# A recurrence beside attention on one core: the framework's scheduler, or the kernel's own list schedule

## The chip, the core and the metric

The kernel runs on one core of a Trainium2 chip. A core has five engines, each with its own queue of instructions that are started in the order of the queue: PE (TensorE, matmuls, with weight loads listed apart as PEld), DVE (VectorE), ACT (ScalarE), POOL (GpSimd) and SP (SyncE, which here only issues DMAs). They meet at semaphores. The metric is device time in microseconds of one execution; lower is better.

## The reference, cut to what matters

The input is eight images of 56 x 56 pixels with 256 channels, fp32. Layer 0 normalizes by groups and runs attention between regions of 8 x 8 pixels: each of an image's 49 regions picks 4 regions by the product of pooled queries and keys, keeps the best 32 of 256 scores for every pixel, takes a softmax over them, adds a depthwise convolution and projects. Layer 1 runs attention in a window of 7 tokens, and then a recurrence over the 3136 tokens of each image:

```python
def step(carry, xs):
    h, c = carry
    xi_t, xf_t, xg_t, xo_t = xs
    i_t = jax.nn.sigmoid(xi_t + h @ V_i)
    f_t = jax.nn.sigmoid(xf_t + h @ V_f)
    g_t = jnp.tanh(xg_t + h @ V_c)
    o_t = jax.nn.sigmoid(xo_t + h @ V_o)
    c_new = h * c + i_t * g_t
    h_new = o_t * jnp.tanh(c_new)
    return ((h_new, c_new), h_new)
```

The new cell state is `h * c + i_t * g_t`, so the gate f is never used: three gates (i, c, o) are computed. All 3136 steps depend on each other; the eight images form the batch of a step. Every residual is added.

## The kernel before, in words

**Order of the program.** An image is seven rows of seven regions; the kernel goes through `rows`, all eight images at row p before row p + 1. For the row at hand it emits seven `region`s, and between them the pieces of a list `todo`: the projection and window attention of the row before it (`project`, `window_attention`), the queries and convolution of the row after it (`queries_and_lepe`) and, while p is 0, the statistics, routing, keys and values of the next image (`norm_and_route`).

**Region (L367 to L448).** SP reads the four chosen places from a table in on-chip memory and issues eight gathers (kg, vg). PE computes scores (`sc`, L399). For each of four groups DVE takes four rounds of the eight largest (`max`, L411) and their removal (`match_replace`, L412), ACT exponentiates (L417), DVE masks and sums (L419), ACT divides (L424), PE transposes (L427), ACT copies (L430), and PE multiplies with the values (`av`, L435).

**Gate terms.** `gates(i)` of `window_attention` multiplies 112 normalized tokens of an image with the input weights (L605), adds the bias on POOL in one instruction of 768 columns (L610), and stores them in memory (`xg`).

**Recurrence (L682 on).** Blocks of 16 steps. The state h lies with channels on partitions, 2 x 8 columns. A step multiplies h, as the stationary operand, with V (L704): the output has the eight images on 8 rows of each of four groups of 32 partitions, so four groups of columns are in work at once. Gates i and c go to one PSUM bank (`r_pic`, 128 columns), gate o to another (`r_po`, 64 columns). ACT has copied the gate terms there beforehand (`place_terms`, L678, two steps at a time), and the matmuls add to them. Then come:

- `r_tic`: DVE transposes i and c (L710); `r_ig`: their tanh on ACT (L712). Sigmoids are made of tanh by halved weights.
- `r_to`, `r_og`: the same for gate o (L714, L716).
- `r_m` and `r_c`: two DVE operations for the new cell state (L719, L724); `r_tc`: its tanh (L726).
- `r_hs`: the new h on DVE (L729); `r_hc`: POOL's product of h and c for the next step (L732).

At the end of a block PE transposes the 16 states (L739), DVE adds the residual (L743), SP stores the result. Terms are loaded eight steps at a time into two buffers (`r_gin`).

**What sets the order.** The Tile framework records the program, and its scheduler reorders the instructions of each engine. The recurrence of a row of tokens can begin when all eight images have stored their gate terms, so its steps are queued when row p, image 1, is reached. `advance` then emits a fixed number of step pieces after each region, at a higher priority (offset 3000):

```python
            rate = -(-len(steps) // (NWIN * nb))
        for qi in range(NWIN):
            ...
            if steps:
                advance(rate)
```

The last 560 steps have no attention left beside them.

Of the kernel before, what the change touches and what calls it, by code (L numbers as in the profile page):

```python
# [8 lines left out]
F32 = mybir.dt.float32  # L9
# [30 lines left out]
SLOTS = 4  # L40
PRIORITY = 3000
# [7 lines left out]


# [5 lines left out]
def _halve(nc, t, views):  # L56


    for v in views:
        for g in (0, 2):  # L60
            w = v.rearrange("p (j g u) -> p j g u", g=GATES, u=UJ)[:, :, g, :]
            nc.vector.tensor_scalar(w, w, 0.5, None, ALU.mult)
# [3 lines left out]
def _layers(ctx: ExitStack, tc, a, out):  # L66
# [96 lines left out]

    def norm_and_route(b, im):
# [42 lines left out]
        def route():  # L209
# [29 lines left out]
            im["kd"] = dram.tile([NREG, P, 2 * S], F32, name=f"kd{b}")  # L239
            im["vd"] = dram.tile([N, C], F32, name=f"vd{b}")  # L240

        def keys_values(p):
# [31 lines left out]
        return (  # L274
            [lambda p=p: stats(p) for p in range(NWIN)]
            + [groups, route]
            + [lambda p=p: keys_values(p) for p in range(NWIN)]
# [9 lines left out]
    def queries_and_lepe(b, p, im, row):  # L287
# [63 lines left out]
        def convolve(m):  # L351
            pl = bank()
            for dx in range(3):
                for g in range(4):
                    nc.tensor.matmul(  # L355
                        pl[g * HD : (g + 1) * HD, :ROW], diag[:, m, dx, g, :],
                        row["vs"][:, m, g, :, dx : dx + W],
                        start=(dx == 0), stop=(dx == 2), skip_group_check=True,
                    )
# [5 lines left out]
        return [  # L365
            queries,
            lambda: (values(0), shift(0)),  # L367
            lambda: (values(1), shift(1)),
            lambda: convolve(0),
            lambda: convolve(1),  # L370
        ]

    def region(n, qi, im, row):


        _, regs = nc.values_load_multi_w_load_instructions(
            im["idx"][n : n + 1, 0:TOPK], engines=[SP], min_val=0, max_val=NREG - 1,
            skip_runtime_bounds_check_because="max_index returns places in 49 columns",
        )
        kg = work.tile([P, TOPK, 2, S], F32, name="kg")  # L380
        vg = work.tile([P, 2, C], F32, name="vg")
        for j, reg in enumerate(regs):
            nc.sync.dma_start(
                kg[:, j].rearrange("p k s -> p (k s)"),
                im["kd"][bass.ds(reg, 1)].rearrange("o p s -> p (o s)"),
            )
            nc.sync.dma_start(
                vg[(j % 2) * S : (j % 2 + 1) * S, j // 2, :], im["vd"][bass.ds(reg * S, S), :]
            )
# [4 lines left out]
        for pair in range(2):  # L394
            both = ps_sc.tile([P, 2, 512], F32, name="sc")
            for g2 in range(2):
                rows = slice((2 * pair + g2) * HD, (2 * pair + g2 + 1) * HD)
                for k in range(2):
                    nc.tensor.matmul(  # L399
                        both[k * S : (k + 1) * S, g2, :KEYS],  # L400
                        row["q"][rows, k, qi * S : (qi + 1) * S],
                        kg[rows, :, k, :], start=True, stop=True,
                    )
# [28 lines left out]
        for k in range(2):  # L432
            for jj in range(2):
                for g in range(4):
                    nc.tensor.matmul(  # L435
                        av[g * HD : (g + 1) * HD, k, :],
                        vg[:, jj, k * P + g * HD : k * P + (g + 1) * HD],
                        probs[g][:, jj, k * S : (k + 1) * S],
                        start=(jj == 0), stop=(jj == 1), skip_group_check=True,
                    )  # L440
# [23 lines left out]
    def project(b, p, im, row):  # L464
# [47 lines left out]
        return [begin] + [lambda i=i: block(i) for i in range(NQB)] + [end]  # L512

    def window_attention(b, p, im, row):
# [83 lines left out]
        def gates(i):  # L598
# [11 lines left out]
            nc.gpsimd.tensor_tensor(gs, gs, bu, ALU.add)  # L610
# [5 lines left out]
        return (  # L616
# [3 lines left out]
            + [lambda i=i: gates(i) for i in range(lo, hi)]  # L620
# [13 lines left out]
    t2 = [dram.tile([QB, nb, C], F32, name=f"t2d{n}") for n in range(NBLK)]  # L634
# [8 lines left out]
    for t in state.values():  # L643
        nc.vector.memset(t, 0.0)
# [235 lines left out]
```

## Time and profile before

| | |
|---|---|
| median of 3 runs | 12276.32 us (12260.72 to 12298.11) |
| profiled execution | 12274.44 us, its span 12272.7 us |
| mean granted PE clock | 0.764 of full |
| busy: PE, DVE, ACT, POOL | 77%, 75%, 44%, 18% |
| first r_hs, last r_hs | 1707.9 us, 12267.9 us |

Busy time is the union of an engine's instructions. Consecutive instructions on one engine overlap a little, and matmuls overlap much, so a mean duration times a count can exceed the busy time. Idle time of an engine counts only where it holds up the chain that ends last. A line of an instruction view gives start, duration, engine, line, operation, output<-inputs, shapes and, in brackets, the idle time before it and who ended it.

### The profile page before, as it was taken

The page shows a single profiled execution, that of the slowest core. Times are in us where ns is not written, and L with a number is a line of the kernel's source. Part 1 is how long each engine was busy: PE and PEld are TensorE (multiplying, and loading weights), DVE is VectorE, ACT ScalarE, POOL GpSimd, SP SyncE. Part 2 cuts the span into 40 slices and gives each one's busy share as a digit, 9 for nine tenths or more (in the row PEclk, how much of TensorE's full clock was granted, in tenths as well). Part 3 has the DMA queues.
Part 4 walks back from the last instruction along what each step waited for, and adds up shares of the span by engine and source line. Part 5 has one row for each costly group of instructions (what it writes and reads, how often), then busy time and mean ns, then how long its engine had stood idle before and what let it go on. Part 6 is the DMA issues. An engine that isn't in the chain of part 4 may idle for free.

```text
span 12272.7 us, 376190 instructions
## 1 busy us (share of the span) xinstructions
PE 9402.1 (77%) x135660; PEld 5455.3 (44%) x135660; DVE 9147.9 (75%) x43038; ACT 5428.8 (44%) x20193; POOL 2178.0 (18%) x6148
## 2 busy tenths in 40 slices
PE   6777778887888887888888887788888888655555
PEld 3344344444444444444444444444444444433333
DVE  5767688888888888888888888888888888533333
ACT  2333344444455444444544444444445444322222
POOL 2222112111122121121211211211112121100000
PEclk8787778777888788787888778887778888755555
DMA  4343322222222222222222222222222222100000
GB/s 135 93 116 99 98 57 61 57 58 58 60 62 57 55 58 55 58 56 54 57 56 59 55 53 59 56 56 57 55 58 56 56 58 53 31 16 17 17 16 15
DMA packets 785586, 705.72 MB, mean 58 GB/s; under 512 B 106403, under 2 KB 755705, under 8 KB 783721
## 3 DMA queue, kind: packets, MB, share of 16 engines
q1 hardware_dynamic: 783720, 681.66, 20.7%
q8 instruction: 1072, 17.56, 0.6%
q14 instruction: 794, 6.50, 0.2%
HBM read 421.58 MB, written 179.83 MB: 49 GB/s over the span
## 4 chain that ended last, share of the span: by engine, by line
PE 48%; DVE 33%; ACT 8%; issue 6%; DMA 2%; POOL 2%; SPq 1%; ACTq 0%; DVEq 0%; POOLq 0%
PE r_pic L704 16%; DVE left L412 9%; DVE top L411 7%; PE r_po L704 6%; PE mm L605 3%; PE pt L427 3%; PE sc L399 3%; DVE r_hs L729 3%; DVE pe L419 3%; DVE r_to L714 3%; PE mm L355 2%; PE av L435 2%; PE mm L532 2%; DVE r_tic L710 2%; DVE r_c L724 2%
## 5 line engine op out<-in xcount | busy, mean ns | idle before, releaser
L704 PE MATMUL r_pic<-r_v,r_hs 128*8 128x128 f32 x50160 | 2599.4, 336 | 1609.2 <-DVE r_hs L729 1593.3
L704 PEld LDWEIGHTS r_pic<-r_v,r_hs 128*8 128x8 f32 x50160 | 1229.0, 100 | 3038.0 <-DVE r_hs L729 2490.0
L710 DVE STREAM_TRANSPOSE r_tic<-r_pic 128x128 f32<-128x128 f32 x3136 | 977.7, 312 | 1439.2 <-PE r_pic L704 1410.2
L712 ACT ACTIVATE r_ig<-r_tic 128x32 f32<-128x32 f32 x3136 | 714.7, 228 | 2999.3 <-DVE r_tic L710 2904.6
L412 DVE MATCH_REPLACE8 left<-top,left 128x256 f32<-128x256 f32 x4704 | 1908.8, 407 | 0.4
L411 DVE MAX8 top<-left 128x8 f32<-128x256 f32 x4704 | 1895.5, 412 | 3.3 <-issue 0.2
L732 POOL TENSOR_TENSOR r_hc<-r_hs,r_c 128x16 f32<-128x16 f32 x3136 | 725.6, 231 | 6255.0 <-DVE r_hs L729 5870.9
L704 PE MATMUL r_po<-r_v,r_hs 128*8 128x64 f32 x50160 | 1655.7, 262 | 0.0
L704 PEld LDWEIGHTS r_po<-r_v,r_hs 128*8 128x8 f32 x50160 | 1334.4, 111 | 161.2 <-issue 0.2
L427 PE MATMUL pt<-ident,pe 128*128 128x128 f32 x3136 | 837.8, 354 | 441.2 <-ACT pe L424 421.5
L399 PE MATMUL sc<-kg,q 32*64 32x256 f32 x6272 | 969.5, 488 | 182.9 <-ACT pe L417 175.1
L417 ACT ACTIVATE pe<-sc,nmax 128x256 f32<-128x256 f32 x1568 | 742.7, 474 | 708.9 <-DVE left L412 473.0
L424 ACT ACTIVATE pe<-pe,inv 128x256 f32<-128x256 f32 x1568 | 787.0, 502 | 549.3 <-DVE inv L423 546.0
L726 ACT ACTIVATE r_tc<-r_c 128x16 f32<-128x16 f32 x3136 | 669.7, 214 | 701.4 <-DVE r_c L724 592.1
L729 DVE SCALAR_TENSOR_TENSOR r_hs<-r_og,r_tc 128x16 f32<-128x16 f32 x3136 | 605.6, 193 | 367.8 <-ACT r_tc L726 347.7
L435 PE MATMUL av<-pts,vg 128*32 128x64 f32 x12544 | 699.2, 264 | 206.8 <-ACT pts L430 167.6
L714 DVE STREAM_TRANSPOSE r_to<-r_po 128x64 f32<-128x64 f32 x3136 | 728.6, 232 | 134.7
L411 DVE MAX8 top<-sc 128x8 f32<-128x256 f32 x1568 | 660.9, 421 | 212.3 <-PE sc L399 172.0
L605 PE MATMUL mm<-wu,xlT 128*112 128x512 f32 (+1 forms) x1792 | 777.9, 557 | 19.5 <-ACT xlT L600 13.9
L430 ACT COPY pts<-pt 128x256 f32<-128x256 f32 x1568 | 579.0, 369 | 468.8 <-PE pt L427 454.9
L427 PEld LDWEIGHTS pt<-ident,pe 128*128 128x128 f32 x3136 | 409.0, 169 | 840.7 <-ACT pe L424 644.3
L415 POOL TENSOR_SCALAR nmax<-top 128x1 f32<-128x1 f32 x1568 | 341.5, 218 | 2299.2 <-DVE top L411 1120.1
(141 smaller groups left out, 14563.1 us busy)
## 6 DMA issues: line engine op xcount, KB each, us to landing
kg<-kd SPq DMA_DIRECT2D x1568, 64.0 KB
vg<-vd SPq DMA_DIRECT2D x1568, 64.0 KB
vshift<-v SPq DMA_DIRECT2D x1344, 58.0 KB
xgd<-gs SPq DMA_DIRECT2D x224, 336.0 KB
r_gin<-xgd SPq DMA_DIRECT2D x1568, 48.0 KB
xchunk<-xt SPq DMA_DIRECT2D x112, 448.0 KB
xn<-xh SPq DMA_DIRECT2D x56, 560.0 KB
x<-x SPq DMA_DIRECT2D x56, 448.0 KB
```

The source lines that it names most:

```text
L399: nc.tensor.matmul(both[k * S : (k + 1) * S, g2, :KEYS], row["q"][rows, k, qi * S : (qi + 1) * S], kg[rows, :, k, :], start=True, stop=True,)
L411: nc.vector.max(top[:, r, :], src)
L412: nc.vector.match_replace(left, top[:, r, :], src, REPLACED)
L417: nc.scalar.activation(pe, sc, AF.Exp, bias=nmax, scale=SCALE)
L424: nc.scalar.activation(pe, pe, AF.Copy, scale=inv)
L427: nc.tensor.transpose(pt[:, jj, :], pe[:, jj * P : (jj + 1) * P], ident)
L435: nc.tensor.matmul(av[g * HD : (g + 1) * HD, k, :], vg[:, jj, k * P + g * HD : k * P + (g + 1) * HD], probs[g][:, jj, k * S : (k + 1) * S] ...
L605: nc.tensor.matmul(pg[:QB, : g - f], xl[:, k, :], wu[:, k, f:g], start=(k == 0), stop=(k == 1),)
L704: nc.tensor.matmul(to[32 * j : 32 * j + nb, :], h[:, k, :], V[:, k, j * GJ + f : j * GJ + f + w], start=False, stop=(k == 1), skip_group_c ...
L710: nc.vector.transpose(tic, pic)
L714: nc.vector.transpose(to_, po)
L729: nc.vector.scalar_tensor_tensor(hn, og, 1.0, tch, ALU.add, ALU.mult)
```

## The change

The kernel no longer leaves the order to the framework. All engine calls of attention and recurrence go to a recorder, `_Plan`, on virtual tiles (`_View`, `_Buf`); its `_depend` derives the dependencies from overlapping boxes, and `run` orders everything by a list schedule on one time line with prices for each instruction (`_time`), then allocates the real tiles and traces the instructions in that order, with the framework's reordering off (`manual_schedule`). PSUM bundles (the matmuls of a recurrence step, of scores, of values, of the convolution) are one entry each (`together`).

- An engine that is free takes the ready entry of lowest rank: the recurrence is rank 0, attention rank 1, in program order within a rank.
- An entry outside the chain is not started if its price would run past the time at which the next chain entry of that engine is expected, plus a slack (`SLACK`).
- The recurrence is recorded as soon as its tokens are (`follow`); `advance`, its rate and its priority are gone, as is the delay of a region's `add` by one region.
- The recurrence itself changes. The three gates share one bank: eight matmuls of 192 columns instead of eight of 128 and eight of 64; one transpose of 192 columns instead of two; one tanh of 48 values instead of 32 and 16, written with stride 3 into a cell buffer; one `tensor_tensor_scan` over 48 values instead of the two DVE operations r_m and r_c. ACT makes half of c (`r_half`), and POOL multiplies it with h into the next cell buffer. Terms are placed in one ACT copy of 384 columns for two steps instead of copies of 256 and 128.
- The gates are ordered c, i, o instead of i, c, o on the host and in `_halve`; POOL's bias addition in `gates` is three instructions of 256 columns.
- A region's table read and its eight gathers are one entry on SP. V is loaded and scaled earlier.

```diff
+HOP = 70
+SLACK = {"PE": 120, "DVE": 60, "ACT": 60, "POOL": 60, "SP": 1000}
+def _time(engine, name, view, reads, args, kw):
+    n = max([_count(v) for v in [view] + reads])
+    if engine == "SP":
+        return 70, 2200
+    if engine == "PE":
+        held = 130 if name == "transpose" else 5 * _count(view) // 3 + 120
+        return held, held + 200
...
+    if engine == "ACT":
+        slow = 80 if kw.get("accum_out") is not None or isinstance(kw.get("scale"), _View) else 0
+        return 5 * n // 7 + 100 + slow, 5 * n // 7 + 200 + slow
+    held = 25 * n // 24 + 60
+    if name == "transpose":
+        return held + 40, held + 120
+    if name == "tensor_tensor_scan":
+        return 2 * n + 60, 2 * n + 170
+    if name == "match_replace":
+        return held + 65, held + 150
...
+    def run(self, tc):
...
+                until = expected(e) + SLACK[e]
+                for i, (rank, op) in enumerate(ready[e]):
+                    if not op.chain and now + op.held > until:
+                        continue
+                    if any(b.free and not self._room(b, made, now) for b in op.takes):
+                        continue
+                    del ready[e][i]
+                    op.start = now
+                    free[e] = now + op.held
+                    done.append(op)
...
+        with tc.manual_schedule():
+            for op in done:
+                for t in op.trace:
+                    t()
...
+        nc.add("SP", [gather], [idx, kd, vd], [kg, vg], 1500, 4500)
...
-            nc.gpsimd.tensor_tensor(gs, gs, bu, ALU.add)
+            for f in range(0, GATES * C, C):
+                nc.gpsimd.tensor_tensor(
+                    gs[:, f : f + C], gs[:, f : f + C], bu[:, f : f + C], ALU.add
+                )
...
-            for to, f, w in ((pic, 0, 2 * UJ), (po, 2 * UJ, UJ)):
-                for k in range(2):
-                    for j in range(J):
-                        nc.tensor.matmul(
-                            to[32 * j : 32 * j + nb, :], h[:, k, :],
-                            V[:, k, j * GJ + f : j * GJ + f + w],
-                            start=False, stop=(k == 1), skip_group_check=True,
-                        )
-            tic = rwork.tile([P, 2 * UJ], F32, name="r_tic")
-            nc.vector.transpose(tic, pic)
...
-            nc.vector.scalar_tensor_tensor(c, hc, 0.5, m, ALU.mult, ALU.add)
+            with nc.rank(0, chain=True):
+                with nc.together(640, 840):
+                    for k in range(2):
+                        for j in range(J):
+                            nc.tensor.matmul(
+                                sum_[32 * j : 32 * j + nb, :], h[:, k, :],
+                                V[:, k, j * GJ : (j + 1) * GJ],
+                                start=False, stop=(k == 1), skip_group_check=True,
+                            )
+                tr = rwork.tile([P, GJ], F32, name="r_tr")
+                nc.vector.transpose(tr, sum_)
+                cell, after = cells[at % 2], cells[(at + 1) % 2]
+                gates = cell[:, 2 : 2 + 3 * CELL].rearrange("p (c b e) -> p c b e", b=nb, e=3)
+                nc.scalar.activation(gates[:, :, :, 0], compact(tr), AF.Tanh)
+                c = rwork.tile([P, 2, nb, 3], F32, name="r_c")
+                nc.vector.tensor_tensor_scan(
+                    c.rearrange("p k b e -> p (k b e)"), cell[:, :CELL],
+                    cell[:, CELL + 2 : 2 * CELL + 2], 0.0, ALU.mult, ALU.add,
+                )
+                tch = rwork.tile([P, 2, nb], F32, name="r_tc")
+                nc.scalar.activation(tch, c[:, :, :, 2], AF.Tanh, scale=0.5)
+                hn = hs[:, :, t, :]
+                nc.vector.scalar_tensor_tensor(
+                    hn, gates[:, 4:6, :, 0], 1.0, tch, ALU.add, ALU.mult
+                )
+            half = rwork.tile([P, 2, nb], F32, name="r_half")
+            nc.scalar.activation(half, c[:, :, :, 2], AF.Copy, scale=0.5)
+            hc = after[:, CELL + 2 : 2 * CELL + 2].rearrange("p (k b e) -> p k b e", b=nb, e=3)
+            nc.gpsimd.tensor_tensor(hc[:, :, :, 2], hn, half, ALU.mult)
+            place_terms(at + 3)
```

## The prediction

> **What bounds the kernel now.** I read the page's busy line, clock line and chain first, then busy time by stretch, then the end of the run instruction by instruction.
>
> ```profile
> PE 9402.1 (77%) x135660; PEld 5455.3 (44%) x135660; DVE 9147.9 (75%) x43038; ACT 5428.8 (44%) x20193; POOL 2178.0 (18%) x6148
> PEclk8787778777888788787888778887778888755555
> PE 48%; DVE 33%; ACT 8%; issue 6%; DMA 2%; POOL 2%; SPq 1%; ACTq 0%; DVEq 0%; POOLq 0%
> ```
>
> No engine is full; the chain runs through PE and DVE. By stretch (columns: length, then PE, PEld, DVE, ACT, POOL busy with counts, clock, DMA share, GB/s):
>
> ```profile
> 0.00:1700.00 1700.00, 1264.83 (x6448) 663.18 (x6448) 1148.18 (x4514) 578.38 (x1408) 353.71 (x677) 0.79 0.36 104
> 3100.00:10610.00 7510.00, 6102.32 (x94660) 3567.03 (x94648) 6184.62 (x29923) 3697.04 (x14030) 1431.92 (x4148) 0.81 0.21 56
> 10610.00:12273.00 1663.00, 888.22 (x18970) 577.98 (x18958) 641.67 (x3029) 486.60 (x2361) 130.77 (x591) 0.50 0.07 16
> ```
>
> Three phases. Until 1700 us there is no recurrence: its first r_hs starts at 1707.9. Until 10610 attention and recurrence share the engines: 448 steps and one row of eight images take 1520 us (step 784 starts at 4617, step 1232 at 6138, step 1680 at 7657), 3.40 us a step, DVE 82% busy. Then the recurrence is alone: 560 steps, the last at 12267.9. One such step:
>
> ```profile
> 11501.10 0.17 DVE L729 SCALAR_TENSOR_TENSOR r_hs<-r_og,r_tc 128x16 f32<-128x16 f32 x1 [0.38 <-ACT r_tc L726]
> 11501.33 1.04 PE L704 MATMUL r_pic<-r_v,r_hs 128*8 128x128 f32 x16 [1.38 <-DVE r_hs L729]
> 11502.14 0.65 PE L704 MATMUL r_po<-r_v,r_hs 128*8 128x64 f32 x16
> 11502.44 0.32 DVE L710 STREAM_TRANSPOSE r_tic<-r_pic 128x128 f32<-128x128 f32 x1 [1.17 <-PE r_pic L704]
> 11502.79 0.23 ACT L712 ACTIVATE r_ig<-r_tic 128x32 f32<-128x32 f32 x1 [1.72 <-DVE r_tic L710]
> 11503.05 0.17 DVE L719 SCALAR_TENSOR_TENSOR r_m<-r_ig 128x16 f32<-128x16 f32 x1
> 11503.33 0.17 DVE L724 SCALAR_TENSOR_TENSOR r_c<-r_hc,r_m 128x16 f32<-128x16 f32 x1
> 11503.59 0.21 ACT L726 ACTIVATE r_tc<-r_c 128x16 f32<-128x16 f32 x1 [0.23 <-DVE r_c L724]
> 11503.84 0.17 DVE L729 SCALAR_TENSOR_TENSOR r_hs<-r_og,r_tc 128x16 f32<-128x16 f32 x1 [0.34 <-ACT r_tc L726]
> ```
>
> The step is a pure latency chain of 2.745 us (r_hs to r_hs); every sixteenth takes 3.43, since L739's transposes go ahead of its matmuls, so 2.81 on average. The output-gate matmuls (r_po) run under the transpose of the other two gates: that split hides them. In the middle phase the step is 0.6 us longer than alone although PE is faster there. Whom do they wait for?
>
> ```profile
> PE r_pic L704 <- DVE r_hs L729: 1593.3, 1479, 4.3
> DVE r_tic L710 <- PE r_pic L704: 1410.2, 1658, 3.6
> ```
>
> PE and DVE wait for each other over this chain: some attention work stands at the wrong place in one in-order queue while the other idles.
>
> [...]
>
> **The change, part by part.** Every price is of the profiled execution (span 12272.7 us, own time 12274.4; the median shown is 12276.3, 2 us more).
>
> *A step alone.* Four column groups work at once: at clock 0.50 groups of four 128-wide records start 213 ns apart, 64-wide ones 107. All 192 columns in one bundle make that 320. The gap after the first group is 175 now, so about 282; the last record starts at 282 + 2 x 320 + 20 = 942 after the first (now 622). It lasts 421 at 128 and 314 at 64, so 528; with the 67 to the reader now, the transpose starts 1537 after PE (now 1110). The chain, in ns:
> - r_hs start to PE: 229, unchanged.
> - PE to transpose: 1537.
> - Transpose: 250 at 64, 317 at 128, so 384 at 192.
> - To tanh: 33 bare. Here the instruction waits for two semaphores, so the order shows a separate wait ahead of it; such a pair costs 93 now (r_c to r_tc). 93.
> - Tanh of 48: 215 at 16, 228 at 32, so 241.
> - To the scan: again a separate wait; r_m to r_c, which has one, takes 104. 104.
> - Scan of 48, not in the trace: a 16-element op lasts 174, [...] I take 258.
> - Tanh and hops to r_hs: 33 + 215 + 33 = 281.
> Sum 3127, range 3010 (one wait free, fast scan) to 3200. That is 0.38 longer than 2.745: merging two vector operations into a scan saves less than exposing the output gate costs. In the new order the block's transposes no longer stand in front of the next bundle. Tail: 560 x 3.13 = 1753 us against 560 x 2.81 = 1572: a loss of 180.
>
> *A step's DVE time under load.* Counted to the next instruction's start in the middle phase, the five present operations take 254, 169, 122, 111, 127 = 783 ns. New: transpose 384 - 75, scan 258 - 75, r_hs 127 = 619. (75 is what back-to-back starts overlap: MAX8 lasts 412, the next starts after 349.) Gain 164 ns.
>
> *The order.* In the changed order of a middle row, step after step, DVE has on average 1.1 attention instructions (377 ns by the trace's start-to-start times) between transpose and scan, 1.3 (404) between scan and r_hs, 3.5 (1092) between r_hs and the next transpose. The waits they lie in, at full clock (PE to transpose then about 940, the streaming halved), are 513, 356 and 1039. Taking the longer of work and wait gap by gap, from that order, gives 2.68 us a step at full clock and 3.19 at half. Attention that does not fit beside the 448 steps is 59 us of DVE (275 in the first row, which has only 336 steps).
> - Clock: [...] at full for 72% of the time, the mean is 2.80.
> - Misfit: ACT's exponentials and PE's matmuls run longer than the plan's prices. The plan prices an exp at 383 ns to its result; the trace has 474. It prices matmuls at full clock. DVE instructions wait in line for both. I add 0.12: 2.92 us.
>
> *Queues.* SP's gather is priced 1.5 us by the plan; a table read and eight DMAs took 5.9 us of SP in the trace. Per row 56 x 5.9 + 192 x 0.63 (vshift) + 224 x 0.35 (r_gin) + about 60 for the rest = 590 us of 1370: not a bound; gathers run up to two regions ahead, r_gin eight steps. If that cover went, the first matmul of a region would wait some 6 us. POOL's gate addition becomes three of about 0.73 (L270's) instead of 1.82: 0.4 x 224 = 90 us on an engine 18% busy, hidden; r_c waited for POOL 12.6 us in all. ACT's scaled copy r_half (about 0.2) stands after r_tc, off the chain; one term copy of 384 (about 0.48) replaces 0.37 + 0.26.
>
> *First phase.* Same work; 1148 us of DVE in 1700 leaves room. The waits there name L488 for PE 135 us, and the xchunk loads about 110. Between 1450 and 1700; I take 1600.
>
> *Sum*, with s the step under load: 1600 + (336 s + 275/0.85) + 4 x (448 s + 65) + (448 s + 15) + 1753 + 5 = 3957 + 2576 s. At 2.92: **11480 us**, 6.5% less. Row: 1373 against 1520; its DVE load is 902 + 448 x 0.62 = 1180, 86% (now 82%).
>
> **Rivals.**
> - *Packed DVE.* The order holds as counted: s = 2.68, first phase 1500: 10760. For: 2.68 is the order's own sum. Against: every misfit of the other engines adds and nothing subtracts.
> - *No use of the order.* s = 3.1, first phase 1700: 12040; the tail eats most of the gain. For: DVE at 82% was what another order reached. Against: that order let matmul groups start in front of the chain; this one keeps PE free for it.
> - *PE becomes the bound; slower.* The plan prices PE at full clock. The attention matmuls between two bundles, counted in the order and priced by the trace's closest starts (256-wide records 215 ns apart, 512-wide 430), come to 1.05 us a step, plus 4 x 160 ns for the bundle. At half clock this is 2.1 + 1.28 = 3.4, with no slack for hand-overs. [...] s = 3.45 and the time is 12840. It decides from s = 3.23. For: alone the grant is 0.50 throughout. Against: under load it is 0.8 already with gaps of this kind.
>
> **How the numbers follow.** Likeliest case 0.64, own range s 2.78 to 3.08, 11050 to 12000. Packed 0.13 (10650 to 11050). No use 0.09, of which 0.02 within 0.3%, about what a measurement of this kernel can tell from no change. PE bound 0.14. The range 10850 to 12300 takes in the first, the third and two thirds of the second. Faster 0.84, same 0.02, slower 0.14.
>
> **What would show it.** A step alone of 3.0 to 3.2 us with no PE work between transpose and r_hs, scan near 258 ns, clock 0.50. Middle rows of 1330 to 1440 us, DVE 84 to 88% busy, clock above 0.81. The wait of the transpose for PE smaller per step than now. I am wrong if rows stay near 1520, if the clock falls below 0.75 in the middle, or if the scan costs 350 or more.

## The result and the profile after

| | before | after |
|---|---|---|
| median | 12275.7 us of 5 runs (12260.72 to 12298.11) | 12173.21 us of 5 runs (12132.97 to 12198.1) |
| ratio, 95% interval | | 0.9916 (0.9892 to 0.9941) |
| profiled execution, its span | 12274.44, 12272.7 us | 12132.97, 12131.1 us |
| mean granted PE clock | 0.764 | 0.778 |
| first r_hs, last r_hs | 1707.9, 12267.9 us | 1717.5, 12126.3 us |

The changed kernel is faster by 0.8%: small, but clear of the noise. The forecast was 6.5%; the sign is right, and seven eighths of the gain are missing. The profiled execution is the fastest of the five, 40 us below their median; sums below are made against it.

The page of the changed kernel, its busy line, clock line and chain. Everything that the recorder issues stands at one line, L274, so the tiles tell the instructions apart:

```profile
PE 8686.0 (72%) x85484; PEld 4051.8 (33%) x85484; DVE 8579.4 (71%) x36771; ACT 5312.2 (44%) x18625; POOL 2264.2 (19%) x6596
...
PEclk8787778887888978888888887878878988555555
...
DVE 38%; PE 35%; ACT 10%; issue 6%; DMA 5%; SPq 4%; POOL 1%; ACTq 0%; DVEq 0%; POOLq 0%
PE r_sum L274 19%; PE mm L274 13%; DVE left L274 10%; DVE top L274 8%; DVE r_tr L274 6%; ACT r_cell L274 5%; DVE r_c L274 5%; SPq L274 3%; DVE r_hs L274 3%; DVE pe L274 2%; ACT pe L274 2%; DMA vshift<-v 2%; ACT r_sum L274 1%; ACT r_tc L274 1%; PE pt L274 1%
```

PE has lost 716 us of busy time and DVE 569, as the smaller instruction counts promise, and the chain now names DVE before PE. But 9% of the chain is DMA and SP's queue (before: 3%), and one tile is named among its DMAs, vshift. By stretch (length, then PE, PEld, DVE, ACT, POOL busy with counts, clock, DMA share, GB/s):

```profile
0.00:1710.00 1710.00, 1212.24 (x6396) 641.12 (x6396) 1118.78 (x4521) 566.38 (x1400) 354.80 (x719) 0.78 0.36 103
3100.00:10340.00 7240.00, 5570.89 (x59654) 2641.47 (x59654) 5858.12 (x25575) 3632.61 (x13001) 1491.98 (x4495) 0.84 0.22 58
10370.00:12131.00 1761.00, 837.98 (x8972) 251.86 (x8970) 468.56 (x1739) 441.75 (x1948) 126.92 (x560) 0.50 0.06 14
```

The middle phase is shorter (7240 us for about the same work), the clock rose from 0.81 to 0.84, yet DVE is 81% busy there, as before (82%) and not the 84 to 88% that was forecast. A step of the recurrence alone, near the end:

```profile
11501.42 0.17 DVE L274 SCALAR_TENSOR_TENSOR r_hs<-r_cell,r_tc 128x16 f32<-128x16 f32 x1 [0.29 <-ACT r_tc L274]
11501.65 1.47 PE L274 MATMUL r_sum<-r_v,r_hs 128*8 128x192 f32 x16 [2.04 <-DVE r_hs L274]
...
11503.19 0.38 DVE L274 STREAM_TRANSPOSE r_tr<-r_sum 128x192 f32<-128x192 f32 x1 [1.59 <-PE r_sum L274]
11503.67 0.27 ACT L274 ACTIVATE r_cell<-r_tr 128x48 f32<-128x48 f32 x1 [2.16 <-DVE r_tr L274]
11504.03 0.26 DVE L274 TENSOR_TENSOR_SCAN r_c<-r_cell 128x48 f32<-128x48 f32 x1 [0.46 <-ACT r_cell L274]
11504.32 0.22 ACT L274 ACTIVATE r_tc<-r_c 128x16 f32<-128x16 f32 x1 [0.39 <-DVE r_c L274]
...
11504.58 0.17 DVE L274 SCALAR_TENSOR_TENSOR r_hs<-r_cell,r_tc 128x16 f32<-128x16 f32 x1 [0.29 <-ACT r_tc L274]
```

From one r_hs to the next are 3.155 us: 3.127 was forecast. The transpose comes 1.54 us after PE and the scan lasts 0.26, as forecast; the 28 ns over are nearly all the tanh of 48 values (267 ns, not 241). So the part of the change that was worked out from single rows came out. What did not come out is the middle. The time from one row's first step to the next row's, and the mean step (row boundaries apart):

| | forecast | after |
|---|---|---|
| first r_hs | 1600 us | 1717.5 us |
| row of 336 steps | 336 x 2.92 + 324 = 1305 us | 1374 us |
| four rows of 448 steps | 1373 us each | 1469, 1457, 1454, 1467 us |
| last row of attention | 1323 us | 1423 us |
| 560 steps alone | 1753 us | 1764 us |
| step under load | 2.92 us | 3.06 to 3.13 us |

The differences are 117, 69, 355, 100 and 11 us; with 2 us after the last r_hs they are, rounding apart, the 653 us between 11480 and the profiled 12133. The waits of the changed kernel (us in total, times, longest) show what holds the middle up:

```profile
DVE r_tr L274 <- PE r_sum L274: 1852.3, 1516, 11.4
...
POOL v L274 <- DMA vshift<-v: 557.5, 37, 26.3
...
PE mm L274 <- DMA vshift<-v: 310.6, 139, 8.3
...
DVE r_c L274 <- POOL r_cell L274: 124.0, 37, 7.7
```

The last three of these waits in the kernel before (of the first, the prediction shows its line):

```profile
PE mm L355 <- DMA vshift<-v: 36.5, 34, 3.1
POOL v L308 <- DMA vshift<-v: 158.9, 9, 23.2
DVE r_c L724 <- POOL r_hc L732: 12.6, 11, 3.3
```

Before, DVE's transpose waited 1410 us for PE, of which 560 x 1.17 = 655 in the steps alone; the rest is 0.29 us for each of 2576 steps under load. After, 560 x 1.59 = 890 of 1852 belong to the steps alone, and 0.37 us a step is left: the wait that should shrink has grown. PE's matmuls waited 36.5 us for vshift before, and wait 310.6 us now. POOL waits 557.5 us for the same transfers (158.9 before), and the scan, which never waited for POOL for long (12.6 us), waits 124 us for it.

vshift is the copy of the values that the convolution (`mm<-vshift,diag`) reads. It takes 24 DMAs of SP for each row of an image, 12 for each half of the channels. One such place, first SP's queue (a bundle's first start and its length):

```profile
5125.63 8.73 SPq L274 DMA_DIRECT2D vshift<-v  x12
5134.46 1.49 SPq L274 DMA_DIRECT2D r_gin<-xgd  x4
5136.06 5.43 SPq L274 DMA_DIRECT2D vshift<-v  x8
5141.61 0.53 SPq L274 DMA_DIRECT2D xn<-xh  x1
5142.23 2.40 SPq L274 DMA_DIRECT2D vshift<-v  x4
```

Twenty-four issues of about 0.59 us each, with four loads of gate terms and one of tokens between them, take SP from 5125.63 to 5144.63. Then PE, DVE and POOL at the same place:

```profile
5146.47 3.69 PE L274 MATMUL mm<-vshift,diag 96*32 96x448 f32 x16 [6.67 <-DMA vshift<-v]
5149.43 1.16 PE L274 MATMUL r_sum<-r_v,r_hs 128*8 128x192 f32 x13
```

```profile
5140.32 0.17 DVE L274 SCALAR_TENSOR_TENSOR r_hs<-r_cell,r_tc 128x16 f32<-128x16 f32 x1
...
5150.85 0.38 DVE L274 STREAM_TRANSPOSE r_tr<-r_sum 128x192 f32<-128x192 f32 x1 [9.22 <-PE r_sum L274]
```

```profile
5147.14 0.18 POOL L274 MEMSET v<- 128x20 f32 x2 [12.43 <-DMA vshift<-v]
5147.31 0.22 POOL L274 TENSOR_TENSOR r_cell<-r_hs,r_half 128x16 f32<-128x16 f32 x1
```

r_hs is there at 5140.3. The recurrence's next matmuls (r_sum) could start 0.23 us later, but ahead of them in PE's queue stand 16 matmuls of the convolution that wait for vshift until 5146.5; r_sum starts at 5149.4, 8.9 us late. That is 5.9 us of waiting and 3.0 us of the convolution's own work, at a granted clock of 0.50 (from 5143.1 to 5149.9 us; 1.00 before and after). DVE has done what stood ahead of its transpose and is idle for 9.2 us. POOL stands at a write to the values' buffer that the same transfers still read, and r_cell, the recurrence's product, stands behind it.

I summed this over the 1790 steps of four rows (steps 785 to 2575), from the start times in the trace: a step's lateness is the start of its first matmul less that of r_hs less 0.23 us. Row boundaries apart, it is 438 us, 0.245 us a step. Convolution matmuls, running or waiting for vshift, stand in front for 273 of them; the fourteen worst, 6.2 to 10.3 us each, all have them in front.

In the plan, SP is free again after 70 ns and a transfer has landed after 2.2 us. Twelve copies are thus believed to have landed 3 us after the first issue. In the trace twelve issues take 7.5 us at best and 8.7 for the first twelve here, and by the trace's semaphore events a copy lands 1.4 us (median) after the end of its issue. From the first issue to the last landing, twelve copies take 8.9 us at best and 9.8 at the median. So the plan lets the convolution start, and puts it into PE's queue, 6 us too early at best and 7 at the median, and an in-order queue then makes the recurrence wait for it.

Here there is a second delay. The sixteen matmuls wait for the last four copies, which stand on SP behind the load of tokens (xn). This load landed at 5146.1, and the four copies between 5146.3 and 5147.0, 2.4 to 3.6 us after their issue.

A long burst does not by itself hold PE up. In the kernel before the bursts were longer under load (14.9 us at the median after 1700 us, 10.1 in the changed kernel), yet of its 36.5 us of PE's waits for vshift 34.2 lie in the first 1600 us. What is new is where the order puts the work that depends on them.

### The profile page after: what moved, and what is told of

The parts are those of the page before. It is cut to its first block, busy times and chain, and to the rows that moved or that the text cites. A ratio compares the mean times of both kernels' runs of the same rounds, so it can differ in the third digit from the quotient of the medians.

```text
span 12131.1 us, 266721 instructions
## 1 busy us (share of the span) xinstructions
PE 8686.0 (72%) x85484; PEld 4051.8 (33%) x85484; DVE 8579.4 (71%) x36771; ACT 5312.2 (44%) x18625; POOL 2264.2 (19%) x6596
## 4 chain that ended last, share of the span: by engine, by line
DVE 38%; PE 35%; ACT 10%; issue 6%; DMA 5%; SPq 4%; POOL 1%; ACTq 0%; DVEq 0%; POOLq 0%
PE r_sum L274 19%; PE mm L274 13%; DVE left L274 10%; DVE top L274 8%; DVE r_tr L274 6%; ACT r_cell L274 5%; DVE r_c L274 5%; SPq L274 3%; DVE r_hs L274 3%; DVE pe L274 2%; ACT pe L274 2%; DMA vshift<-v 2%; ACT r_sum L274 1%; ACT r_tc L274 1%; PE pt L274 1%
## 5 line engine op out<-in xcount | busy, mean ns | idle before, releaser
L274 PE MATMUL r_sum<-r_v,r_hs 128*8 128x192 f32 x50160 | 3454.2, 401 | 2242.9 <-DVE r_hs L274 2190.7
L274 PEld LDWEIGHTS r_sum<-r_v,r_hs 128*8 128x8 f32 x50160 | 1239.2, 99 | 4298.7 <-DVE r_hs L274 3501.0
L274 DVE STREAM_TRANSPOSE r_tr<-r_sum 128x192 f32<-128x192 f32 x3136 | 1183.1, 377 | 1877.3 <-PE r_sum L274 1852.3
L274 ACT ACTIVATE r_cell<-r_tr 128x48 f32<-128x48 f32 x3136 | 834.9, 266 | 3340.4 <-DVE r_tr L274 3050.8
L274 POOL TENSOR_TENSOR r_cell<-r_hs,r_half 128x16 f32<-128x16 f32 x3136 | 735.1, 234 | 6543.1 <-DVE r_hs L274 5214.7
L274 DVE MATCH_REPLACE8 left<-top,left 128x256 f32<-128x256 f32 x4704 | 1909.5, 407 | 1.5 <-issue 1.5
L274 DVE MAX8 top<-left 128x8 f32<-128x256 f32 x4704 | 1884.9, 408 | 1.8
L274 DVE TENSOR_TENSOR_SCAN r_c<-r_cell 128x48 f32<-128x48 f32 x3136 | 846.8, 270 | 710.9 <-ACT r_cell L274 418.1
L274 ACT ACTIVATE pe<-sc,nmax 128x256 f32<-128x256 f32 x1568 | 733.2, 473 | 785.6 <-DVE left L274 538.6
L274 ACT ACTIVATE pe<-pe,inv 128x256 f32<-128x256 f32 x1568 | 782.5, 501 | 500.8 <-DVE inv L274 495.5
L274 PE MATMUL pt<-ident,pe 128*128 128x128 f32 x3136 | 773.3, 332 | 315.1 <-ACT pe L274 290.0
L274 ACT ACTIVATE r_tc<-r_c 128x16 f32<-128x16 f32 x3136 | 700.2, 223 | 577.7 <-DVE r_c L274 556.5
L274 PE MATMUL mm<-vshift,diag 96*32 96x448 f32 x2688 | 646.2, 776 | 365.6 <-DMA vshift<-v 310.6
L274 DVE MAX8 top<-sc 128x8 f32<-128x256 f32 x1568 | 638.2, 415 | 240.5 <-PE sc L274 230.8
L274 PE MATMUL mm<-wu,xlT 128*112 128x256 f32 (+1 forms) x1792 | 795.4, 567 | 14.2 <-ACT xlT L274 14.0
L274 ACT COPY r_sum<-r_gin 128x384 f32<-128x384 f32 x1568 | 774.9, 495 | 44.2 <-DMA r_gin<-xgd 42.0
L274 PE MATMUL sc<-kg,q 32*64 32x256 f32 x6272 | 620.7, 471 | 147.0 <-ACT pe L274 111.7
L274 DVE SCALAR_TENSOR_TENSOR pe<-left,pe 128x256 f32<-128x256 f32 x1568 | 658.6, 422 | 75.5 <-ACT pe L274 73.8
L274 PEld LDWEIGHTS pt<-ident,pe 128*128 128x128 f32 x3136 | 410.7, 162 | 877.3 <-ACT pe L274 516.7
L274 DVE SCALAR_TENSOR_TENSOR r_hs<-r_cell,r_tc 128x16 f32<-128x16 f32 x3136 | 558.5, 178 | 185.1 <-ACT r_tc L274 172.5
L274 ACT COPY pts<-pt 128x256 f32<-128x256 f32 x1568 | 568.5, 363 | 204.7 <-PE pt L274 200.4
L274 ACT ACTIVATE r_half<-r_c 128x16 f32<-128x16 f32 x3136 | 652.4, 208 | 0.0
```

Of the source, the lines that this page charges most:

```text
L274: method(*[v.real() if isinstance(v, _View) else v for v in args], **{k: v.real() if isinstance(v, _View) else v for k, v in kw.items()},)
```

## The experiments

The main theory, A, was this: the plan's price for SP's DMAs is too small, and the work that it therefore puts too early stands in front of the recurrence. If A is right, the true price brings the forecast's own numbers. Rivals: the merged step or the list schedule is itself worth less than was forecast; or what counts is SP's occupancy, not the time at which a burst has landed. Ratios are to the kernel before, with 95% intervals.

| run | what | median us | ratio |
|---|---|---|---|
| | after | 12173.21 | 0.9916 (0.9892 to 0.9941) |
| e1_sp_price | all of SP's DMAs at their traced price | 11521.94 | 0.9383 (0.9366 to 0.9400) |
| e2_vshift_price | vshift alone at its traced price | 11672.66 | 0.9500 (0.9481 to 0.9519) |
| e9_vshift_late | vshift: 70 ns of SP, but landing 10 us later | 11764.43 | 0.9589 (0.9571 to 0.9607) |
| e7_twelve_shifts | half as many copies, twice as large, old prices | 12112.15 | 0.9871 (0.9852 to 0.9891) |
| e3_framework_merged | the framework's order with the merged step | 12918.36 | 1.0514 (1.0491 to 1.0536) |
| e4_plan_split | the plan with the step of before | 12596.48 | 1.0252 (1.0231 to 1.0272) |
| e8_sp_split | e1's prices with the step of before | 11831.33 | 0.9642 (0.9623 to 0.9662) |
| e6_pe_act_price | e1's prices, and PE and ACT too | 11442.31 | 0.9328 (0.9313 to 0.9344) |
| e5_sp_hybrid | e1's prices, step of before where it is alone | 11315.77 | 0.9223 (0.9208 to 0.9239) |
| e11_best | e6's prices, step of before where it is alone | 11242.11 | 0.9160 (0.9144 to 0.9177) |

Each expectation was written before its run; where it uses letters, A is the theory above and another letter the rival that it words beside it.

**e1_sp_price.** The plan's prices for SP, each with the time at which the transfer is believed to land:

```diff
     if engine == "SP":
-        return 70, 2200
+        held = 640 if view.buf.name == "vshift" else 420
+        return held, held + 2200
...
-        nc.add("SP", [gather], [idx, kd, vd], [kg, vg], 1500, 4500)
+        nc.add("SP", [gather], [idx, kd, vd], [kg, vg], 6000, 8200)
```

> Only the plan's prices for SP are changed, to what the traces show: 640 ns of SP for a vshift DMA (was 70) and 420 for any other, 6000 for a region's gathers (was 1500), landing 2200 later. Theory A (SP's price): the plan believes that 24 shifts cost SP 1.7 us where they cost 15, so it puts the convolution's matmuls into PE's queue too early, and the recurrence's matmuls stand behind them; the trace after has 273 us of that in four rows (0.15 us a step) and 75 us in the first phase. Then PE's wait for vshift falls below 60 us in all (311 now), a step under load goes from 3.10 to 2.95 or less, a row from 1460 to about 1390, the whole from about 12170 to 11650 (11500 to 11800). Theory B (prices of PE and ACT, clock): the convolution only stands where something else would have stood; the gain is under 100 us.

Measured: 11521.94 us. First r_hs at 1598.6, rows of 1381, 1370, 1379 and 1372 us, step 2.92, 560 steps alone 1764.7 us: against 1600, 1373, 2.92 and 1753. The waits of this run (its recorder's line is L275) and its stretches:

```profile
DVE r_tr L275 <- PE r_sum L275: 1489.0, 1496, 7.0
...
POOL v L275 <- DMA vshift<-v: 59.8, 21, 8.5
...
PEld mm L275 <- DMA vshift<-v: 14.0, 18, 1.8
...
PE mm L275 <- DMA vshift<-v: 6.5, 12, 1.5
```

```profile
0.00:1595.00 1595.00, 1150.59 (x6404) 630.35 (x6404) 1133.20 (x4529) 570.34 (x1402) 358.44 (x723) 0.80 0.39 110
3000.00:9700.00 6700.00, 5279.01 (x58694) 2465.34 (x58683) 5771.12 (x25172) 3582.93 (x12794) 1471.84 (x4431) 0.85 0.24 61
9730.00:11494.00 1764.00, 839.47 (x8990) 252.26 (x8988) 470.26 (x1743) 442.93 (x1953) 127.23 (x561) 0.50 0.06 14
```

PE's matmuls wait 6.5 us for vshift instead of 310.6 (their weight loads 14.0 instead of 146.8), POOL 60 instead of 557.5, and the scan's wait for POOL fell from 124 to 2.6 us. DVE is 86% busy in the middle. A step's lateness at PE fell from 0.245 to 0.124 us, and the convolution's share of it from 273 to 74 us. Together with the scan's wait for POOL (121 us less over 2576 steps, 0.05) this is 0.17 of the 0.18 us by which the step got shorter. A holds: with the same number of instructions on every engine, an order made with traced prices for SP is 651 us faster.

**e2_vshift_price.** The price of vshift alone:

```diff
-        return 70, 2200
+        return (640, 2840) if view.buf.name == "vshift" else (70, 2200)
```

> As the one before, but only the vshift DMA is priced anew (640 ns of SP), the gathers and all other DMAs as in the changed kernel. Theory A: nearly all of the gain comes from this price, within 80 us of the kernel with all SP prices. If the gathers' price matters as much (a region's first matmuls placed too early), it stays over 150 us behind. Theory B: under 100 us of gain.

Measured: 11672.66 us, so this one price brings 500 of the 651 us. The step is 2.97 us (average of the rows; 2.91 to 3.00), the first r_hs at 1620.7. The other 150 us come from the prices of the gathers and loads, more than was expected of them. In part they still act through vshift: PE's matmuls wait 30.1 us for it here and their weight loads 50.5, against 6.5 and 14.0 in e1_sp_price.

**e9_vshift_late.** Occupancy and landing taken apart:

```diff
-        return 70, 2200
+        return (70, 10000) if view.buf.name == "vshift" else (70, 2200)
```

> The changed kernel with one price altered: the shifted copies (vshift) hold SP for 70 ns in the plan as before, but are believed to land 10 us after their issue instead of 2.2; every other price stays. The theory that the convolution's matmuls are placed too early because of the time at which the copies are believed to land: this works as well as the true price of 640 ns did, 11600 to 11750 us, PE's waits for vshift below 60 us. The rival, that SP's occupancy decides (the plan believes SP free and puts other DMAs and gathers too early): about the changed kernel's 12110 to 12200 us. Something between, 11800 to 12050, would say that both count.

Measured: 11764.43 us, 14 us above the first theory's range and 350 below the rival's; PE's matmuls wait 56.9 us for vshift, as the first theory had it. The stretches differ. Under load the step is 2.96 us and the six rows take 8255 us together, against 8279 in e2_vshift_price: there the believed landing alone does all that the full price does. But the first r_hs comes at 1714.3 us, as in the changed kernel (1717.5), and not at 1620.7: the late landing alone does not help the first phase. Until 1600 us POOL stands for 147 us at the values' buffer, which vshift still reads (199 in the changed kernel, 9 in e2_vshift_price). SP's occupancy can be the reason, or that 10 us are too short for POOL, which needs all twenty-four copies (24 x 0.6 = 14 us of issue); these runs do not separate the two. The waits of the whole run lie between those of the changed kernel and of e1_sp_price:

```profile
DVE r_tr L274 <- PE r_sum L274: 1564.1, 1493, 8.2
...
POOL v L274 <- DMA vshift<-v: 230.4, 33, 20.0
...
PE mm L274 <- DMA vshift<-v: 56.9, 55, 5.5
```

**e7_twelve_shifts.** The plan's prices as they were, but each copy covers both halves of the channels (so the copies are recorded after the values of both halves, which the cut leaves out):

```diff
-                        row["vs"][dy * HD : (dy + 1) * HD, m, g],
-                        row["v"][g * HD : (g + 1) * HD, m, dy : dy + R, :],
+                        row["vs"][dy * HD : (dy + 1) * HD, :, g],
+                        row["v"][g * HD : (g + 1) * HD, :, dy : dy + R, :],
```

> The changed kernel with its prices as they are (70 ns), but the shifts of both channel halves in one DMA: 12 instead of 24 a row of an image, each twice as large. If theory A holds, it is SP's real time behind the wrong price that hurts; about 7 us of it go per row of an image (12 x 0.6), the wait for vshift on PE falls by half or more, and half or more of the gain of the right price comes without it: 11800 to 11950. If the transfers themselves, not their issue, were late, nothing changes: 12100 to 12200.

Measured: 12112.15 us, 61 us less than the changed kernel; the gain that was expected did not come. A copy twice as large costs SP 632 ns instead of 597 in the mean, so SP's time for vshift nearly halves. But now each half of the convolution needs all twelve, which are issued over 8 to 10 us, where it needed twelve issued over 7.5 to 9 before; the plan still believes in 3 us.

```profile
PE mm L274 <- DMA vshift<-v: 316.8, 54, 13.5
POOL v L274 <- DMA vshift<-v: 271.6, 23, 19.5
DVE r_c L274 <- POOL r_cell L274: 203.6, 38, 10.0
```

PE waits as long as before, in fewer and longer waits (the longest 13.5 us, before 8.3), and the rows are those of the changed kernel; only the first phase is 33 us shorter. The time is in the range of the rival, that the transfers themselves are late, but e1_sp_price and e2_vshift_price leave the transfers as they are and win. So less time on SP does not help by itself while the believed landing stays wrong.

**e3_framework_merged.** The kernel before, with its recurrence function replaced by the new one, and the gates in the new order; the framework orders it:

```diff
-            tic = rwork.tile([P, 2 * UJ], F32, name="r_tic")
-            nc.vector.transpose(tic, pic)
...
+            tr = rwork.tile([P, GJ], F32, name="r_tr")
+            nc.vector.transpose(tr, sum_)
...
+            nc.vector.tensor_tensor_scan(
```

> The kernel before, order by the framework's scheduler with the fixed rate, but with the changed recurrence step (192 columns at once, scan). This is the change's second half alone. From the traces the step alone is 3.16 us (2.75 before), so the tail costs 560 x 0.41 = 230 us less the block transposes' share, about 200 more. Under load the step loses 0.16 us of DVE work but its chain is longer; theory C (latency rules the middle phase): rows 1520 to 1570, total 12480 to 12750. Theory D (DVE load rules it): rows 1450, total about 12050 to 12150.

Measured: 12918.36 us, 642 us slower than before, beyond what I expected. Its middle and its end:

```profile
3080.00:10900.00 7820.00, 6322.01 (x58586) 2794.91 (x58589) 5907.96 (x25379) 3607.89 (x12760) 1406.95 (x4101) 0.78 0.20 53
11120.00:12906.00 1786.00, 836.56 (x8966) 251.41 (x8966) 471.60 (x1740) 441.56 (x1947) 125.97 (x557) 0.50 0.05 13
```

The step alone is 3.20 us on average, and the end takes 1791 us, 1569 in the kernel before; under load the step is 3.58 us instead of 3.39, with DVE 76% busy (82% before) and the clock at 0.78 (0.81). In this order the smaller vector work of a step brought nothing where a row is full: DVE idles more. The first phase and the first row (1385 us, before 1395) are no longer than before; each full row is 63 to 104 us longer, and the end 222. That the longer chain is the cause fits, but only for the end is it shown.

**e4_plan_split and e8_sp_split.** The reverse: the plan orders the step of before, with the plan's prices for SP or with e1's. Its matmuls are two bundles, and the operations on the output gate are of the recurrence's rank but not of its chain:

```diff
-            with nc.rank(0, chain=True):
-                with nc.together(640, 840):
...
+            with nc.rank(0, chain=True):
+                with nc.together(430, 630):
+                    matmuls(pic, 0, 2 * UJ)
+            with nc.rank(0):
+                with nc.together(215, 415):
+                    matmuls(po, 2 * UJ, UJ)
```

> The changed kernel's plan with the recurrence step of the kernel before (two bundles in two banks, two transposes, m and c instead of the scan); the change's first half alone. The tail returns to 560 x 2.75 = 1540 us without the block transposes in front, 225 less than the changed kernel. Under load: theory C, chain shorter by about 0.2 at full clock, rows no longer than the changed kernel's 1460, total 11850 to 11950. Theory D: 0.16 us more DVE work and five more meetings of engines a step, rows 1540, total 12350 to 12450.

> The plan with SP priced as traced and the recurrence step of the kernel before throughout. If the 12596 of the plan with the old step came from SP's price, this is about 600 faster: 11950 to 12050. If it came from DVE's load (0.16 us a step more, attention left over at the end of every row), rows stay above 1500: 12300 to 12500.

Measured: 12596.48 and 11831.33 us, the first slower than either theory had it and the second faster: I had underrated what SP's prices do to the old step too. With SP's true prices the step of before runs under load at its own 2.75 us, which the merged step never reached at those prices (2.92), and 765 us fall away. Yet it loses to the merged step by 309 us. One row of it, its 447 steps and then what follows before the next row's first step:

```profile
2969.70:4199.10 1229.40, 954.68 (x17923) 591.11 (x17912) 1044.10 (x5119) 635.31 (x2567) 254.70 (x791) 0.82 0.22 56
4199.20:4438.10 238.90, 175.27 (x1220) 91.13 (x1218) 218.92 (x960) 103.59 (x267) 48.58 (x113) 0.75 0.26 70
```

Attention that did not fit beside the steps is done afterwards, with no recurrence beside it: 239 us a row (267 to 270 in e4_plan_split) instead of 65 to 76. DVE's work for a row was 902 us of attention and 783 ns for each step of before, 1253 us together (the two stretches show 1263), more than the 448 x 2.75 = 1232 us that the steps last. The merged step's 619 ns make 1180, which fits. The merged step saves 11831 - 11522 = 309 us in all although its end is 199 us longer (1765 and 1566 us), so 508 us while attention runs. These sums point to its smaller vector work, which counts in a good order; but the two steps differ in their matmul bundles too, and no run changes the vector work alone.

**e6_pe_act_price.** e1's prices, PE's durations and bundles a fifth longer, and ACT's nearer to the trace (468 ns to an exp's result, where the changed kernel's trace has 473):

```diff
-        return held, held + 200
+        held = held * 6 // 5
+        return held, held + 220
...
-        return 5 * n // 7 + 100 + slow, 5 * n // 7 + 200 + slow
+        slow += 85 if kw.get("bias") is not None else 0
+        return 5 * n // 6 + 100 + slow, 5 * n // 6 + 170 + slow
```

> SP priced as traced, and PE and ACT as well: every PE price a fifth higher (mean granted clock under load 0.84), ACT at 0.83 ns an element and 85 more for a bias read from memory. If the rest of the misfit is price (prediction: 0.12 us a step), the recurrence's matmuls are late less often (0.124 us a step now) and rows go from 1371 to about 1340: 11320 (11250 to 11400). If the misfit lies in what no fixed price can hold (a clock that changes between half and full), nothing is won or dearer prices leave gaps: 11480 to 11620.

Measured: 11442.31 us, 80 less than e1_sp_price (67 by the ratios, as the profiled executions have it) and short of what was expected. The step is 2.80 us, what the forecast had without its misfit term; the lateness at PE is 0.07 us. Over 2576 steps that is 0.12 x 2576 = 309 us. But in shorter steps less attention fits: what is left over at the ends of the six rows (311, 76, 65, 65, 65 and 40 us in e1_sp_price) is now 329, 104, 108, 107, 107 and 111 us, 244 us more, and takes most of it back, so what is won is 65 us. The middle:

```profile
3000.00:9600.00 6600.00, 5125.17 (x58421) 2389.50 (x58418) 5725.23 (x25056) 3550.59 (x12724) 1476.15 (x4414) 0.90 0.24 62
```

**e5_sp_hybrid and e11_best.** The merged step until step 2576, the step of before in the last 560, where nothing runs beside it:

```diff
+            if at >= SPLIT:
+                return split_step(t, at, hs, h)
```

> SP priced as traced, and the recurrence step of the kernel before (two bundles, m and c) in the last 560 steps alone, where nothing stands beside the recurrence; the scan step up to there. Theory: alone the step is latency, 3.157 us with the scan and 2.745 without, so the tail goes from 1765 to about 1545 us and nothing else moves: 11300 (11250 to 11340). If the transposes at the end of a block stand in front of the matmuls again, as in the run with the plan and the old step throughout (2.80 a step), the tail is 1568 and the time 11325. Rival: the switch costs the plan its tail; no gain.

> The prices of SP, PE and ACT as measured, the merged step while attention runs, and the old split step in the last 560 steps. If the two gains add: 11442 us with the merged step throughout, less the 206 us that the old step in the tail saved with SP's prices alone, is 11236 us (range 11200 to 11290), with a tail of about 1567 us. Rival: the row at the change of step leaves vector work over, or the clock falls, and the saving shrinks to 100 us: about 11340.

Measured: 11315.77 and 11242.11 us, both as expected: the gains add. The stretches of e11_best:

```profile
0.00:1598.00 1598.00, 1166.10 (x6460) 638.44 (x6460) 1128.14 (x4543) 570.01 (x1409) 359.14 (x724) 0.78 0.39 110
3000.00:9500.00 6500.00, 5067.64 (x57616) 2353.36 (x57620) 5623.41 (x24627) 3493.34 (x12536) 1449.04 (x4346) 0.89 0.24 62
9670.00:11240.00 1570.00, 849.36 (x17978) 542.04 (x17976) 604.08 (x2869) 465.62 (x2243) 128.11 (x566) 0.51 0.07 17
```

Its last 560 steps take 1565 us instead of 1764, its rows are those of e6_pe_act_price (1358 to 1366 us). It is the fastest kernel of the study, 8.4% below the kernel before and 7.6% below the changed one (11242 / 12173).

## Why the prediction was right and wrong

- **A step alone, and the end.** Right: 3.155 us against 3.127, 1764 us against 1753, with the parts as forecast (matmuls to transpose 1.54 us, a scan of 258 ns at the median). The 258, and the faster scan in the lower end of the range, were assumptions that the trace of before, which has no scan, did not show. Two readings on the way were loose and did no harm. A step of 3.43 us in sixteen makes 2.79 on average; the 2.81 that were used are what the trace has, with some other longer steps. And the MAX8 pair that is given for an overlap of 75 ns overlaps by 63; in this trace a transpose overlaps by 76 and a scan by 82, as was assumed.
- **"Queues": the step that failed.** I added SP's times per row, 192 x 0.63 us for vshift among them, compared the sum of 590 us with 1370, and wrote "not a bound". That is a statement on throughput. The plan's price for SP also tells it when a burst has landed, and with it where PE's, POOL's and DVE's dependent instructions go in their queues. Twelve copies were believed to land within 3 us and take 9.8 at the median. The recurrence's matmuls were 0.245 us late in each step, 273 of the 438 us behind the convolution, and the step was 3.10 us instead of 2.92. I asked what would happen if the gathers' cover went, and not what the plan would do with a landing that it believes too early. For one copy the issue is the smaller part here (0.59 of the 2.0 us from its start to landing, at the median); for twelve in line it is nearly all: 7.5 us or more of issue, then 1.4 us until the last has landed. e1_sp_price shows that with this step mended the step under load comes out at the forecast's 2.92 us and the time 42 us above 11480, e9_vshift_late that under load it is the believed landing, e7_twelve_shifts that less time on SP alone brings 61 us.
- **The misfit term.** I sized it 0.12 us for ACT and PE; measured against the 2.80 of the order it is 0.30. With SP's prices right it is 0.12, and with PE's and ACT's repriced too (e6_pe_act_price) it is 0.00, though most of the time comes back at the ends of rows. Part of that is the clock, by an estimate: 0.90 was granted then, which is 1.00 for four fifths of the time and 0.50 for the rest, if only these two occur as in the traces of before and after; the forecast's 2.68 and 3.19 us then give 2.77. The size of 0.12 was a choice, so that e1_sp_price meets 2.92 so closely is in part luck; that PE's and ACT's prices are behind it is shown for both together, not for each.
- **The first phase.** 1717.5 us against 1600. The 1600 were chosen out of 1450 to 1700; with SP's prices right it is 1598.6, which is luck as to the digit. The price of vshift alone brings 1620.7, so the cause is the same price; whether it acts through SP's occupancy or through a landing that is later still than 10 us is open.
- **The leftovers and DVE.** Right but for the last row: 325 us after the first row (forecast 324), and 77, 67, 69 and 69 us later, a step of 3 us included (forecast 65), but 57 after the last, where 15 were taken. DVE's 81% goes with the waits, and e1_sp_price shows the 86% of the forecast.
- **The clock.** 0.84 in the middle (above 0.81, as forecast) and 0.85 in e1_sp_price. In the changed kernel's trace the clock is 1.00 for 68% of the middle and 0.50 for the rest (before: 63%); by the same two values 0.85 is 70%. The 72% I took was an estimate. That a shorter row would raise the clock was an assumption.
- **The rivals.** "No use of the order" came closest: the right step, 3.1 us, and 12040 us, but the wrong reason. Against it I wrote that this order keeps PE free for the chain. It does so in the plan's time, not in the chip's. "PE becomes the bound" did not come: the clock in the middle rose from 0.81 to 0.84. That it would stay at half beside attention was an assumption, which no trace showed. "Packed DVE" was not reached with the merged step by any run (s = 2.80 at best), and e6_pe_act_price suggests why it is hard to reach: DVE's work for a row is 1180 us, and 448 steps of 2.68 us are 1201. Of the three signs of being wrong none came; but the rows of 1454 to 1469 us and DVE's 81% miss what would have shown the forecast right.

What stays open: which of the other DMAs the 150 us between e2_vshift_price and e1_sp_price belong to; what in vshift's price the first phase needs; how e6_pe_act_price's gain divides between PE and ACT; and whether it is the merged step's vector work that e8_sp_split lacks.

## What to carry to other kernels

An order that is fixed beforehand can be undone by one wrong price (here 70 ns for 590, worth 500 us of 12173), and a price for a queue does two things: it says when the queue is free again, and when the work that depends on it may be put into other in-order queues. Check both, and for a burst of transfers check the landing of the last one against the trace; a comparison of sums per row cannot see it. An operation merged to save engine time and one split to shorten a latency chain are each right in their own stretch (here the merged step saved 508 us while attention ran and cost 199 us at the end): merge where the engine is full, split where the chain is alone.

## What the runs showed of the hardware

- SP's issue of a vshift copy, 32 partitions of 58 KB in all, lasts 588 ns at the median, and one of twice the size 597 (means 597 and 632): twice the size costs SP 9 ns more at the median, 35 in the mean. The copy lands 1.4 us after the end of its issue at the median.
- A scan of 48 fp32 elements lasts 258 ns at the median (mean 270), about 84 more than the 174 of a 16-element vector operation.
- With PE as busy (78% of the middle in e6_pe_act_price, 79% in e1_sp_price) the granted clock was 0.90 in one and 0.85 in the other. Only prices, and so the order, differ. The busy share alone does not give the clock. Nor is it a clean measure of the load, since a matmul takes longer at the lower clock (a convolution matmul of the changed kernel 0.54 us at 1.00 and 0.95 at 0.50, at the median); what the clock follows here is not settled.
- In the traces of before and after the granted clock is 1.00 or 0.50 at any time. In the kernel before, groups of four 128-wide matmuls of a step start 109 ns apart at 1.00 and 213 at 0.50, at the median.
